# One layer of masked attention on one core: earlier order of tiles, q loads from GpSimd, later output adds, and five more tiles turned on VectorE

## The chip, the core and the metric

The kernel runs on one core of a Trainium2 chip. Its engines run side by side, each in the order of its own queue: TensorE (PE; its weight loads are PEld), VectorE (DVE), ScalarE (ACT), GpSimd (POOL) and SyncE (SP), which here only issues transfers. The metric is the device time of one execution in microseconds, as the median of several runs.

## The reference

One layer over 2708 rows of width 1024, float32. `adj` is a random 0/1 matrix with a density of 0.0014771, so that a row has four edges in the mean.

```python
h = jnp.maximum(_layernorm(x, axis=-1), 0.0)
q = h @ W_q.T + b_q
k = h @ W_k.T + b_k
v = h @ W_v.T + b_v
z = scale * (q @ k.T)
spare_z = z * adj
spare_z = jnp.where(spare_z == 0.0, -10000.0, spare_z)
attn = jax.nn.softmax(spare_z, axis=1)
out = x + jax.nn.relu(attn @ v)
```

## The kernel before

**Algebra.** W_q and W_k are multiplied into one matrix M, so that a score is (h M + b) · h', and W_v is applied after the weighted sum: a row's output is relu(u W_v + b_v) + x, where u is the weighted sum of its neighbours' h rows. Both big products (h M and u W_v) run by Strassen's scheme in Winograd's form on 512-wide halves: seven products for a pair of tiles instead of eight.

**Tiles and units.** The 2708 rows are sorted by their number of edges, within the first 1024 rows (tiles 0 to 7) and within the rest (tiles 8 to 21). A tile is 128 rows. K[t] is the number of edge slots of tile t. The hosts, tiles 0 and 8, would need 15 slots; they keep 8 (WIDE), and the slots past the 8th of their first rows make up tile 21 (SECOND), half of it for each host, with 7 slots. SECOND's sum goes through memory (`v_dram`) and is added in the host's last step.

TensorE's main loop goes over 20 units of two tiles. Units 0 to 9 are the q pairs (0,1) to (18,19). Units 10 to 19 are the output pairs, in the order in which attention finishes tiles (`order`, line 989). Tile 8 is left over (`alone`) and comes last, with four products. `multiply` (line 1044) has seven places, `after(0)` to `after(6)`, between the products of a unit; a place is written here as (unit, i). The products are s2, a12, s4, s3, then a11 and s1 of the **next** unit (`between`, `opened`), then a22. The operands s1 to s4 of the next unit are written by VectorE at (n, 2), as `put` in `blocks` (line 711).

**Turning.** A matmul needs the tile's transpose. A tile is turned in one of two ways. In the plain way TensorE does eight 128x128 transposes into PSUM (`half_turned`, line 410), and ScalarE or VectorE takes them out. A tile in `faced_tiles` goes another way: ScalarE rearranges its sum u (line 944), it is written to `u_dram`, read back in four transfers with the 32-row quarters exchanged (`by_quarters`, line 695), and VectorE transposes 32x32 blocks, a half tile in one instruction (`faces`, line 703). A tile that is not faced is either kept in SBUF (`held`) or also goes through `u_dram`. Before the change tiles 6, 5, 4, 3, 2, 0, 20, 7, 17 and 13 are faced.

**Attention.** It runs on VectorE beside the products, as a generator (`attention`, line 959) that is advanced by a planned number of microseconds, `share`, at each place (line 1277). For each slot of a tile GpSimd gathers 128 rows of h by index (line 610), VectorE multiplies with q and sums (`scores`, line 863), ScalarE takes the exponential, and VectorE adds the weighted rows into u (`sums`, line 923; ScalarE does the first slot, line 912). The gathers use 11 slots of SBUF, and two more in M from unit 10 on. A tile's q is loaded into `pq` in `fetch` (line 820): by a gather from GpSimd for tiles 0 to 7, from the SP queue for the others (line 833).

VectorE's order is written out by hand (`manual_schedule`): it is the order in which the program says things, so a planned step stands in one queue with the operands that TensorE waits for. The orders on ScalarE, GpSimd and SP are made by the framework's scheduler in the attention stage.

**W_v.** It takes the place of M when the last q products are done. Its four blocks are loaded from the SP queue (line 1259), and VectorE forms four differences of 128x2048 in T (line 1263), at places of units 9 and 10.

**Output.** `o_results` (line 1111) writes relu(u W_v + b_v) into y; GpSimd adds the x rows by an indirect transfer (`add_x`, line 1106) right after ScalarE's last write, and `send` scatters the tile to the output when the next add has been issued (line 808).

Of the kernel before, what the change touches and what calls it, by code (L numbers as in the profile page):

```python
# [18 lines left out]
P = 128  # L19
# [46 lines left out]
def tile_preln_masked_attention(  # L66
# [28 lines left out]
    HP = P // 2  # L95
    VK = K[0] - WIDE
    assert K[0] == K[EARLY] and K[SECOND] == 0 and WIDE + VK <= SLOTS
# [68 lines left out]
    mass = const.tile([P, 2], FT, name="mass")  # L166
# [17 lines left out]
    for t in HOSTS:  # L184
        nc.vector.memset(cap[:HP, t:t + 1], float(WIDE + VK))
# [448 lines left out]
    def reload(lo, hi):  # L634

        full = min(hi, FULL)
        src = tab_dram[lo >= EARLY]
        loads = [(nc.gpsimd if lo >= EARLY else nc.sync).dma_start(ptab[:, lo:full, :], src[:(full - lo) * P, :].rearrange("(t p) w -> p t w", p=P))]
        if hi > FULL:
            loads.append(nc.gpsimd.dma_start(ptab[:REST, FULL, SLOTS:], src[(FULL - lo) * P:, SLOTS:]))  # L640
        part = slice(HP, P) if lo >= EARLY else slice(0, HP)
        loads.append((nc.gpsimd if lo >= EARLY else nc.sync).dma_start(
            ptab[part, SECOND, 0:SLOTS + 1 - WIDE], src[0:HP, WIDE:SLOTS + 1]))
# [171 lines left out]
    def ask(t):  # L815

        g_of[t] = []
        wanted.extend((t, s) for s in range(K[t]))

    def fetch(t):  # L820
# [7 lines left out]
        if t == SECOND:  # L828
            assert EARLY in formed
            gather(tq[t][:HP], q_dram[:, :], t, SLOTS - WIDE, HP)  # L830
            nc.sync.dma_start(tq[t][HP:], q_late[:HP, :])
        elif t >= EARLY:
            nc.sync.dma_start(tq[t], q_late[(t - EARLY) * P:(t - EARLY + 1) * P, :])
# [5 lines left out]
    def fill():  # L839
        while wanted and free:  # L840
            t, s = wanted.pop(0)
            g = free.pop(0)
            if s == K[t]:
                half = slice(HOSTS.index(t) * HP, (HOSTS.index(t) + 1) * HP)
                nc.gpsimd.dma_start(g[:HP], v_dram[half, :])
# [29 lines left out]
    def weights(t):  # L875
# [7 lines left out]
        if t == SECOND:  # L883
# [4 lines left out]
            nc.sync.dma_start(mass[:HP, 1:2], mass[HP:, 0:1])  # L888
# [15 lines left out]
        else:  # L904
            with tc.issue_after(chain[-1].ins):
                nc.vector.scalar_tensor_tensor(w[:, :k], w[:, :k], 1.0, ok, op0=ALU.mult, op1=ALU.mult, accum_out=m[:, 1:2])
                if t in HOSTS:
                    second = HOSTS.index(t)
                    nc.vector.tensor_add(m[:HP, 1:2], m[:HP, 1:2], mass[:HP, second:second + 1])
# [4 lines left out]
            if t in HOSTS:  # L914
                assert whole_second
                wanted.insert(0, (t, k))
        us[t] = u, coef, m

    def sums(t):
        u, coef, m = us.pop(t)  # L920
        for s in range(0 if t in EMPTY else 1, K[t]):
            fill()
            chained(lambda: nc.vector.scalar_tensor_tensor(  # L923
# [4 lines left out]
        if t in HOSTS:  # L928
            chained(lambda: nc.vector.scalar_tensor_tensor(
                u[:HP], g_of[t][K[t]][:HP], m[:HP, 3:4], u[:HP], op0=ALU.mult, op1=ALU.add))  # L930
# [9 lines left out]
        if now < [unit - 2, 2] and unit <= len(q_pairs) + 4:  # L940
            faced_tiles.add(t)
        if t in faced_tiles:
# [16 lines left out]
    def attention(order):  # L959
# [11 lines left out]
        for i, t in enumerate(order):  # L971
            nxt = after[i]
            ahead = nxt is not None and K[t] + K[nxt] <= HIGH + 1
# [40 lines left out]

    def opened(n):
# [8 lines left out]
        products.append(add_block(Z, ops["s1"], T[:, 0]))  # L1024
# [19 lines left out]
    def multiply(n, results, after):  # L1044
# [7 lines left out]
        products.append(add_block(Y, ops["s2"], T[:, 1]))  # L1052
# [58 lines left out]
    def o_results(ta, tb):  # L1111
# [12 lines left out]
        def c12(Z, u2):  # L1124
# [5 lines left out]
            send(add_x(ya, ta))  # L1130
            sent.append((ya, ta))

        def c21(Y):
            nc.scalar.activation(yb[:, lo], Y, AF.Relu)  # L1134
            send(add_x(yb, tb))
            sent.append((yb, tb))
# [29 lines left out]
    sent = []  # L1166

    def send(behind):

        while sent:  # L1170
            y, t = sent.pop(0)
            with tc.issue_after(behind.ins):
                scatter(y, t, P)

    def tail(t):
        n = tiles[t][1]
        y = work.tile([P, D], FT, tag="q", name=f"y_{t}", bufs=4)
        nc.sync.dma_start(y[:n], tail_dram.to_broadcast([n, D]))
        add_x(y, t, n)
        scatter(y, t, n)  # L1180
# [9 lines left out]
    units = [("q",) + p for p in q_pairs] + [("o",) + p for p in o_pairs]  # L1190

# [19 lines left out]
    last_q = len(q_pairs) - 1  # L1211
# [13 lines left out]
    for n, unit in enumerate(units):  # L1225
# [7 lines left out]
        share = 20.9 / 7  # L1233
# [5 lines left out]
        def after(i):  # L1239
            now[1] = i  # L1240
            if (n, i) in steps_ahead:
                follow(steps_ahead[n, i])
            if (n, i) == (2, 5):
                owe(8)
                owe(9)
                rows_of[FIRST] = load_rows(units[FIRST])
# [9 lines left out]
            for at, place, src in (((-1, 0), b12, of_wv(0, 1)), ((0, 0), b11, of_wv(0, 0)), ((0, 2), T[:, 1], of_wv(1, 1)),  # L1256
# [3 lines left out]
            for at, place, a, b in (((0, 2), T[:, 0], b12, b11), ((0, 4), T[:, 1], T[:, 1], T[:, 0]),  # L1260
                                    ((1, 0), T[:, 2], b22, b12), ((1, 1), T[:, 3], b21, T[:, 1])):
# [16 lines left out]
            if nxt is not None:  # L1278
# [14 lines left out]
                if i == (2 if n in (FIRST, last_q) else 4) and n + 2 > FIRST and n + 2 < len(units) and n + 2 not in rows_of:  # L1293
# [71 lines left out]
    add_block(Z, uT[:, 0:4, :], T[:, 0])  # L1365
# [189 lines left out]
```

## Time and profile before

| | |
|---|---|
| median of 3 runs | 643.78 us (642.85, 643.78, 648.3) |
| the profiled execution, its own time | 639.94 us |
| span of its records | 638.1 us |
| mean granted TensorE clock | 0.997 |
| DMA | 176.96 MB, mean 277 GB/s |

The profile is one execution of its own, 3.84 us below the median; 1.84 us of its time lie outside the span. A row of a view names line, engine, operation and tiles; "out<-in" are the program's names with buffer numbers left out. Start times are microseconds from the span's first record. In a PE row one 128x512 float32 matmul leaves two records, so that a product of four matmuls shows as x8; a 128x128 transpose leaves one.

### The profile page before, as it was taken

What the parts mean: (1) busy time and instruction counts of PE and PEld (TensorE: products, weight loads), DVE (VectorE), ACT (ScalarE), POOL (GpSimd) and SP (SyncE); (2) the same over time, 40 slices, a digit from 0 to 9 for tenths busy, and PEclk for the clock granted to TensorE, in tenths of its full rate; (3) what the DMA queues carried; (4) which work ended last, traced back from release to release, by engine and by line L of the source; (5) the groups of instructions that cost most, each with busy time, mean ns of one, the idle gap of its engine ahead of it and who ended that gap; (6) DMA issues with size and microseconds to landing.
All of it is one profiled execution on the core that took longest, in us unless ns stands there. A gap on an engine that the chain in (4) does not pass through costs nothing.

```text
span 638.1 us, 6156 instructions
## 1 busy us (share of the span) xinstructions
PE 627.8 (98%) x1651; PEld 317.9 (50%) x1651; DVE 522.4 (82%) x1016; ACT 283.6 (44%) x423; POOL 360.2 (56%) x383
## 2 busy tenths in 40 slices
PE   9999999999999999999999999999999999999994
PEld 5777766444444444444444444444444444444441
DVE  5999888997997625999888999999999889989121
ACT  3538985849667533424342144343342432333200
POOL 2639960885768357565651663476466878633311
PEclk9999999999999999999999999999999999999998
DMA  8999997598796439996798998999999999853631
GB/s 335 407 362 321 342 351 286 200 323 330 255 379 231 171 95 317 327 323 223 233 299 289 290 414 222 295 344 311 363 382 325 325 290 291 266 145 77 187 119 50
DMA packets 60192, 176.96 MB, mean 277 GB/s; under 512 B 9799, under 2 KB 15255, under 8 KB 59512
## 3 DMA queue, kind: packets, MB, share of 16 engines
q0 software_dynamic: 25136, 78.41, 39.4%
q1 hardware_dynamic: 29514, 78.61, 35.0%
q10 hardware_dynamic: 5502, 19.48, 7.8%
q8 instruction: 15, 0.25, 0.2%
q14 instruction: 25, 0.20, 0.1%
HBM read 145.65 MB, written 40.74 MB: 292 GB/s over the span
## 4 chain that ended last, share of the span: by engine, by line
PE 90%; issue 4%; POOL 2%; DMA 2%; DVE 1%; POOLq 0%; ACT 0%; ACTq 0%; DVEq 0%
PE ps L1010 40%; PE psy L1010 29%; PE ps_y L476 6%; PE ps_x L476 4%; PE ps_z L476 4%; PE pt L415 4%; POOL g L610 2%; DMA v_dram<-u 1%; DMA M<-h_dram,tab 1%; PE ps_y L511 1%; DVE junk L863 0%; PE ps_h L1218 0%; PE ps_v L594 0%; DVE u L923 0%; DVE s L722 0%
## 5 line engine op out<-in xcount | busy, mean ns | idle before, releaser
L610 POOL DMA_INDIRECT g<-h_dram,tab x94 | 120.2, 1278 | 79.9 <-DVE u L923 30.0
L1010 PE MATMUL psy<-wlow,s 128*128 128x512 f32 x320 | 144.0, 592 | 0.0
L1010 PE MATMUL ps<-M,a 128*128 128x512 f32 x320 | 144.0, 593 | 0.0
L863 DVE SCALAR_TENSOR_TENSOR junk<-g,pq 128x1024 uint8<-128x1024 f32 x93 | 113.8, 1224 | 13.4 <-DMA g<-h_dram,tab 10.4
L1010 PEld LDWEIGHTS ps<-M,a 128*128 128x128 f32 x320 | 59.7, 190 | 70.4 <-issue 69.1
L923 DVE SCALAR_TENSOR_TENSOR u<-g,coef,u 128x1024 f32<-128x1024 f32 x69 | 88.4, 1281 | 7.0 <-ACT u L912 5.8
L1010 PEld LDWEIGHTS psy<-wlow,s 128*128 128x128 f32 x320 | 59.6, 190 | 69.2 <-issue 69.0
L389 DVE FIND_INDEX8 at<-ones,adj 128x8 uint32<-128x685 f32 (+1 forms) x88 | 74.5, 864 | 0.0
L1010 PE MATMUL ps<-wlow,s 128*128 128x512 f32 x160 | 72.0, 593 | 0.4 <-DVE s L722 0.4
L1010 PE MATMUL ps<-M,s 128*128 128x512 f32 x160 | 72.1, 592 | 0.0
L1010 PE MATMUL psy<-wlow,a 128*128 128x512 f32 x160 | 72.0, 593 | 0.0
L368 ACT ACTIVATE sized<-adj 128x2708 uint8<-128x2708 f32 (+1 forms) x22 | 54.3, 2467 | 7.4 <-DMA adj<-in_adj_dram 6.1
L298 POOL TENSOR_TENSOR hsum<-hsum,x 128x256 f32<-128x256 f32 (+1 forms) x56 | 38.6, 732 | 26.2 <-DVE wlow L444 22.5
L1109 POOL DMA_INDIRECT y<-in_x_dram,tab x19 | 34.2, 1798 | 28.9 <-ACT y L1134 12.1
L1010 PEld LDWEIGHTS ps<-wlow,s 128*128 128x128 f32 x160 | 30.3, 190 | 38.9 <-issue 38.5
L1010 PEld LDWEIGHTS psy<-wlow,a 128*128 128x128 f32 x160 | 30.3, 190 | 38.5 <-issue 37.3
L1010 PEld LDWEIGHTS ps<-M,s 128*128 128x128 f32 x160 | 30.3, 190 | 38.1 <-issue 37.4
L808 POOL DMA_INDIRECT out_dram<-y,tab x21 | 27.4, 1306 | 32.0 <-DMA y<-in_x_dram,tab 15.8
L912 ACT ACTIVATE u<-g,coef 128x1024 f32<-128x1024 f32 x18 | 20.7, 1149 | 35.8 <-DVE coef L911 35.6
L276 ACT ACTIVATE x<-x,r 128x1024 f32<-128x1024 f32 (+1 forms) x22 | 25.9, 1232 | 6.6 <-POOL r L266 6.6
L722 DVE TENSOR_TENSOR s<-a,pt 128x512 f32<-128x512 f32 x30 | 19.2, 681 | 10.9 <-ACT a L718 10.9
L476 PE MATMUL ps_y<-wlow 128*128 128x512 f32 x64 | 27.6, 592 | 0.0
(251 smaller groups left out, 843.3 us busy)
## 6 DMA issues: line engine op xcount, KB each, us to landing
adj<-in_adj_dram SPq DMA_DIRECT2D x21, 1354.0 KB, 11.5
x<-in_x_dram SPq DMA_DIRECT2D x21, 512.0 KB, 8.2
h_dram<-x ACTq DMA_DIRECT2D x21, 512.0 KB, 7.4
q_late<-q SPq DMA_DIRECT2D x12, 512.0 KB, 5.1
pq<-q_late SPq DMA_DIRECT2D x12, 512.0 KB, 6.6
u_dram<-v ACTq DMA_DIRECT2D x10, 512.0 KB, 6.4
or<-u_dram SPq DMA_DIRECT2D x40, 128.0 KB, 7.0
M<-in_wv_dram SPq DMA_DIRECT2D x4, 1024.0 KB, 8.4
```

Source lines behind the costliest of these rows:

```text
L276: nc.scalar.activation(xs[i][:n], xs[i][:n], AF.Relu, bias=r[:n, 4, i:i + 1], scale=r[:n, 3, i:i + 1])
L298: small.append(nc.gpsimd.tensor_add(hsum[:n, cols], hsum[:n, cols], xt[:n, cols]))
L368: nc.scalar.activation(sized[:n], a[:n, :, :PW], AF.Abs, accum_out=total[:n, t:t + 1])
L389: nc.vector.max_index(at[:n, k - first_k, g, :], ones[:n, 0:8], a[:n, g, :])
L415: nc.tensor.transpose(pt[:, c, :], xt[:, k * P:(k + 1) * P], ident)
L476: mm = nc.tensor.matmul(bank, a_tile(o + H * a[0], a[1], i), b(o), start=first and o == 0, stop=(o == H - 1), skip_group_check=True)
L610: return nc.gpsimd.indirect_dma_start(out=dst, out_offset=None, in_=src, in_offset=off, bounds_check=N - 1, oob_is_err=False)
L808: to = nc.gpsimd.indirect_dma_start(out=out, out_offset=bass.IndirectOffsetOnAxis(ap=ptab.bitcast(U32)[:n, t, SLOTS:SLOTS + 1], axis=0), i ...
L863: chained(lambda: nc.vector.scalar_tensor_tensor(junk, g_of[t][s], 1.0, tq[t], op0=ALU.mult, op1=ALU.mult, accum_out=zall[:, t, s:s + 1]))
L923: chained(lambda: nc.vector.scalar_tensor_tensor(u, g_of[t][s], coef[:, s:s + 1], u, op0=ALU.mult, op1=ALU.add))
L1010: mm = nc.tensor.matmul(bank, a[:, c, :], b[:, c, :], start=False, stop=(c == 3), skip_group_check=True)
L1109: return nc.gpsimd.indirect_dma_start(out=y[:n], out_offset=None, in_=x, in_offset=off, compute_op=ALU.add)
```

## The change

Seven edits are made together.

1. **Four slots.** SECOND has 4 slots instead of 7. A host's overflow is put in two parts (`OVER`): slots 8 to 11 of its first 48 or 60 rows, and slots 12 to 15 of its first 8 or 12. The second part's sum is added into the first one's by an accumulating transfer from GpSimd, issued in the host's sums; the host's `v_dram` row tile is asked for with its other slots.
2. **Order.** SECOND comes before tile 3 instead of before tile 0; the later tiles go 13, 17, 12, 18, 11, 19, 10, 15 instead of 17, 13, 18, 12, 19, 11, 15, 10.
3. **q loads.** `pq` of tiles 8 to 19 is loaded from GpSimd instead of SP.
4. **q rows.** The h rows of a q unit are gathered at (n-2, 2) instead of (n-2, 4), and the first two tiles' gathers stand ahead of two additions on GpSimd.
5. **Shares.** 22.2 us of planned steps per unit before unit 9, 17.6 in units 9 and 10, 21.2 afterwards, instead of 20.9 throughout (less 2.3 for each faced tile of the next unit, as before).
6. **Output adds.** `add_x` is issued at (n, 5) and (n+1, 1) instead of directly behind ScalarE's last write of a tile, and a tile is scattered when one more add has been issued.
7. **Turning and W_v.** Tiles 12, 18, 16, 9 and 8 are faced too, so 15 in all. Two of the four places in T are exchanged for W_v, and two of its blocks are loaded at (8, 6).

```diff
-    VK = K[0] - WIDE
+    VK = 4
+    OVER = ((48, 0), (8, 48)), ((60, 56), (12, 116))
...
         elif t >= EARLY:
-            nc.sync.dma_start(tq[t], q_late[(t - EARLY) * P:(t - EARLY + 1) * P, :])
+            nc.gpsimd.dma_start(tq[t], q_late[(t - EARLY) * P:(t - EARLY + 1) * P, :])
...
         for s in range(0 if t in EMPTY else 1, K[t]):
             fill()
+            if t in HOSTS and s == K[t] // 2 + 1:
+                rows, at = OVER[HOSTS.index(t)][1]
+                nc.gpsimd.dma_start(g_of[t][K[t]][:rows], v_dram[at:at + rows, :], accum_op=ALU.add)
...
-        if now < [unit - 2, 2] and unit <= len(q_pairs) + 4:
+        if now < [unit - 2, 2] and unit <= len(q_pairs) + 5 or unit >= len(units) - 1:
             faced_tiles.add(t)
...
-    order = [6, 5, 4, 3, 2, 0, 20, 7, 17, 13, 18, 12, 19, 11, 15, 10, 14, 1, 16, 9, 8]
+    order = [6, 5, 4, 3, 2, 0, 20, 7, 13, 17, 12, 18, 11, 19, 10, 15, 14, 1, 16, 9, 8]
-    stream = attention(order[:order.index(0)] + [SECOND] + order[order.index(0):])
+    stream = attention(order[:order.index(3)] + [SECOND] + order[order.index(3):])
...
+    def t_of(n, k):
+        return T[:, (1, 0, 2, 3)[k] if n > last_q else k]
...
-            send(add_x(ya, ta))
-            sent.append((ya, ta))
+            due.append((now[0], 5, ya, ta))
...
-            send(add_x(yb, tb))
-            sent.append((yb, tb))
+            due.append((now[0] + 1, 1, yb, tb))
...
+    def add_due():
+        while due and due[0][:2] <= tuple(now):
+            y, t = due.pop(0)[2:]
+            send(add_x(y, t), 1)
+            sent.append((y, t, P))
...
-        share = 20.9 / 7
+        share = (22.2 if n < last_q else 17.6 if n < last_q + 2 else 21.2) / 7
...
-            for at, place, src in (((-1, 0), b12, of_wv(0, 1)), ((0, 0), b11, of_wv(0, 0)), ((0, 2), T[:, 1], of_wv(1, 1)),
+            for at, place, src in (((-1, 0), b12, of_wv(0, 1)), ((-1, 6), b11, of_wv(0, 0)), ((-1, 6), T[:, 0], of_wv(1, 1)),
                                    ((0, 3), b21, of_wv(1, 0)), ((0, 4), b22, of_wv(1, 1))):
...
-            for at, place, a, b in (((0, 2), T[:, 0], b12, b11), ((0, 4), T[:, 1], T[:, 1], T[:, 0]),
-                                    ((1, 0), T[:, 2], b22, b12), ((1, 1), T[:, 3], b21, T[:, 1])):
+            for at, place, a, b in (((0, 2), T[:, 1], b12, b11), ((0, 4), T[:, 0], T[:, 0], T[:, 1]),
+                                    ((1, 1), T[:, 2], b22, b12), ((1, 2), T[:, 3], b21, T[:, 0])):
...
-                if i == (2 if n in (FIRST, last_q) else 4) and n + 2 > FIRST and n + 2 < len(units) and n + 2 not in rows_of:
+                if i == (2 if FIRST <= n < last_q - 1 or n == last_q else 4) and n + 2 > FIRST and n + 2 < len(units) and n + 2 not in rows_of:
...
             if nxt is None and i == 1:
+                uT = work.tile([P, D], FT, tag="hT", name="T_alone", bufs=2).rearrange("p (c q) -> p c q", q=P)
+                faces(uT, single["rows"], 0, DC)
+                single["turned"] = uT
+            if n == len(units) - 2 and i == 6:
                 while alone not in done:
                     advance(1.0)
-                r, = load_rows(("o", alone))
-                single["turned"] = turned(r, "alone")
+                single["rows"], = load_rows(("o", alone))
```

More of the change, by code (lines that the diff above doesn't have):

```diff
@@ L94, in tile_preln_masked_attention @@
     SECOND = NT - 1
-    HP = P // 2
-    VK = K[0] - WIDE
-    assert K[0] == K[EARLY] and K[SECOND] == 0 and WIDE + VK <= SLOTS
+    VK = 4
+    OVER = ((48, 0), (8, 48)), ((60, 56), (12, 116))
+    assert K[0] == K[EARLY] <= WIDE + 2 * VK == SLOTS and K[SECOND] == 0
+    assert sum(rows for host in OVER for rows, at in host) == P
     for t in HOSTS:
@@ L817, in ask @@
         g_of[t] = []
-        wanted.extend((t, s) for s in range(K[t]))
+        wanted.extend((t, s) for s in range(K[t] + (t in HOSTS)))
     def fetch(t):
@@ L843, in fill @@
             if s == K[t]:
-                half = slice(HOSTS.index(t) * HP, (HOSTS.index(t) + 1) * HP)
-                nc.gpsimd.dma_start(g[:HP], v_dram[half, :])
+                assert whole_second
+                rows, at = OVER[HOSTS.index(t)][0]
+                nc.gpsimd.dma_start(g[:rows], v_dram[at:at + rows, :])
             else:
@@ L972, in attention @@
             nxt = after[i]
-            ahead = nxt is not None and K[t] + K[nxt] <= HIGH + 1
+            ahead = nxt is not None and K[t] + (t in HOSTS) + K[nxt] <= HIGH + 1
             part = scores(nxt, after[i + 1]) if nxt is not None else iter(())
@@ L1240, in after @@
             now[1] = i
+            add_due()
             if (n, i) in steps_ahead:
```

63 lines of the change are left out of this document (36 added, 27 removed).

## The prediction

> **What bounds the kernel now.** I read the page first: its span, its busy times and the chain of work that ended last.
>
> ```profile
> span 638.1 us, 6156 instructions
> PE 627.8 (98%) x1651; PEld 317.9 (50%) x1651; DVE 522.4 (82%) x1016; ACT 283.6 (44%) x423; POOL 360.2 (56%) x383
> PE 90%; issue 4%; POOL 2%; DMA 2%; DVE 1%; POOLq 0%; ACT 0%; ACTq 0%; DVEq 0%
> ```
>
> TensorE is busy for 627.8 of 638.1 us and makes 90% of the chain. Busy ends are modelled for matmuls, so I asked what TensorE waited for (in total, times, longest):
>
> ```profile
> PE ps_y L511 <- POOL hsum L121: 1.2, 1, 1.2
> PE ps L1010 <- DVE s L722: 0.4, 1, 0.4
> ```
>
> That is 1.6 us in all, 1.2 of it before the first product. So nearly all of the time is TensorE's own list of work, and an edit pays only as far as it shortens that list or a wait in it. The end of the chain shows what follows the last product:
>
> ```profile
> 618.97 10.42 PE ps L1010 x24
> 629.41 0.70 DVE y_alone L1371
> 630.65 0.70 POOL out_dram L1355
> ```
>
> From 629.4 to 638.1, 8.7 us are an addition, a scatter of half a tile and its landing. The change touches none of the three. The other edits act before that, beside the products. The gain can therefore be at most the removed work on TensorE plus 0.4 us.
>
> **The turned tiles.** The timeline of TensorE in unit 17, which has two tiles turned by it:
>
> ```profile
> 545.64 1.04 PE L415 MATMUL pt<-ident,u 128*128 128x128 f32 x8
> 546.52 3.60 PE L1010 MATMUL psy<-wlow,s 128*128 128x512 f32 x8
> 549.95 1.04 PE L415 MATMUL pt<-ident,u 128*128 128x128 f32 x8
> 550.83 3.60 PE L1010 MATMUL ps<-M,a 128*128 128x512 f32 x8
> 554.26 3.60 PE L1010 MATMUL ps<-M,s 128*128 128x512 f32 x8
> ```
>
> Starts tell what the list costs, since the durations overlap: eight transposes take 546.52 - 545.64 = 0.88 us, a product 3.43. The groups of transposes in the output units, by form:
>
> ```profile
> L415 PE MATMUL pt<-ident,u 128*128 128x128 f32 x56 | 7.3, 273 | 0.0
> L415 PE MATMUL pt<-ident,or 128*128 128x128 f32 x32 | 4.2, 273 | 0.0
> ```
>
> 88 transposes are eleven tiles. The built program of the change has 40 fewer, the five tiles 12, 18, 16, 9 and 8. 5 x 0.88 = **4.4 us less on TensorE**. The mean of 273 ns holds the latency of one, not its place in the list; whoever multiplies it by 40 gets 10.9 us (a rival below). [...]
>
> **What the five tiles cost elsewhere.** A faced tile takes two block transposes on VectorE, 5 x 2 x 0.69 = 6.9 us; three slots fewer in SECOND save 3 x (1.22 + 0.08 + 1.28) = 7.7 us there, the 0.08 being the read of the sum. So VectorE's list is as long as before (the rows, with the idle time in front of a group and who ended it, behind the second bar):
>
> ```profile
> L863 DVE SCALAR_TENSOR_TENSOR junk<-g,pq 128x1024 uint8<-128x1024 f32 x93 | 113.8, 1224 | 13.4 <-DMA g<-h_dram,tab 10.4 <-DMA pq<-q_dram,tab 1.0 <-DMA pq<-q_late 0.2
> L863 DVE DVE_READ_ACCUMULATOR junk<-g,pq 128x1 f32 x93 | 7.6, 81 | 0.0
> L923 DVE SCALAR_TENSOR_TENSOR u<-g,coef,u 128x1024 f32<-128x1024 f32 x69 | 88.4, 1281 | 7.0 <-ACT u L912 5.8
> L923 DVE SCALAR_TENSOR_TENSOR u<-g,w,u 128x1024 f32<-128x1024 f32 x6 | 7.7, 1282 | 1.5 <-ACT u L889 1.4
> L705 DVE STREAM_TRANSPOSE a<-or 128x512 f32<-128x512 f32 x15 | 10.0, 694 | 1.0 <-DMA or<-u_dram 1.0
> ```
>
> Tiles 12 and 18 went through memory before; 16, 9 and 8 were kept, and now take a copy, a write and a read in quarters. The tightest is tile 8. Its last sum and the product that needs it turned:
>
> ```profile
> 586.70 1.28 DVE L929 SCALAR_TENSOR_TENSOR u<-g,m,u 64x1024 f32<-64x1024 f32 x1
> 611.82 3.60 PE L1010 MATMUL ps<-M,T_alone 128*128 128x512 f32 x8
> ```
>
> The transfers (median us to landing), and the group of the copies:
>
> ```profile
> u_dram<-v ACTq DMA_DIRECT2D x10, 512.0 KB, 6.4
> or<-u_dram SPq DMA_DIRECT2D x40, 128.0 KB, 7.0
> pq<-q_late SPq DMA_DIRECT2D x12, 512.0 KB, 6.6
> pq<-q_dram,tab POOLq DMA_INDIRECT x9, 6.9
> ```
>
> ```profile
> L944 ACT COPY v<-u 128x1024 f32<-128x1024 f32 x10 | 10.5, 1046 | 22.6 <-DVE u L923 20.7 <-DMA g<-h_dram,tab 1.8
> ```
>
> 588.0 + 1.0 + 6.4 + 7.0 + 1.4 (two faces) = 603.8, against 611.8 - 4.4 = 607.4: 3.6 us of cover, and VectorE has nothing else due in unit 19 before the first product's end. I cost it at nothing; were the cover gone, a microsecond of lateness would be one on TensorE.
>
> **VectorE's lead.** TensorE takes s1 of the next unit late in a unit; the time from VectorE's write to that product is the lead. Units 10 and 11, from the two timelines:
>
> ```profile
> 356.49 0.69 DVE L722 TENSOR_TENSOR s<-a,s 128x512 f32<-128x512 f32 x1
> 364.26 3.60 PE L1010 MATMUL ps<-wlow,s 128*128 128x512 f32 x8
> 388.19 0.69 DVE L722 TENSOR_TENSOR s<-a,s 128x512 f32<-128x512 f32 x1
> 389.03 3.67 PE L1010 MATMUL ps<-wlow,s 128*128 128x512 f32 x8 [0.36 <-DVE s L722]
> ```
>
> The lead is 364.26 - 357.18 = 7.1 us for unit 10, and 0.1 for unit 11, where the one wait is. The four W_v differences bring it down. I counted the 1024-wide attention steps that VectorE's order puts between the s1 of unit 6 and that of units 10 and 11: 59 and 71 before, 62 and 71 after. So the new shares move three steps (3 x 1.28 = 3.8 us) ahead of unit 10 and none net ahead of unit 11. SECOND's sums, no longer right behind its weights, lose the 1.4 us of idle time (ScalarE's L889 above). The leads become 7.1 - 3.8 + 1.4 = 4.7 and 0.1 + 1.4 = 1.5, before any new wait.
>
> **The W_v load is such a wait.** The SP queue's issues, the landing times of the W_v loads, and VectorE's first difference:
>
> ```profile
> 340.43 0.33 SPq L1259 DMA_DIRECT2D M<-in_wv_dram  x1
> 348.25 0.33 SPq L1084 DMA_DIRECT2D q_late<-q  x1
> 350.73 0.33 SPq L1259 DMA_DIRECT2D wlow<-in_wv_dram  x1
> ```
>
> ```profile
> DMA to landing us min/median/max: 5.2/5.4/11.6
> ```
>
> ```profile
> 351.76 2.28 DVE L1263 TENSOR_TENSOR wlow<-M 128x2048 f32<-128x2048 f32 x1
> ```
>
> Before, the block b11 went out at 340.4, ahead of a q store that waits for unit 8's last product. In the built order of the change it stands behind that store, and ScalarE's copy of tile 0's sum (1.0) stands ahead of the copy that the store waits for: an issue at 350.7 by my estimate (348.25 and a few tenths at the least). Landing takes 5.2 to 11.6, so 353.9 to 362.3, most likely 356.1. The first difference would start at 351.8 + 3.8 - 1.4 = 354.2. So VectorE waits 0 to 8.1 us, most likely 1.9; queued behind it are its own sums and the operands of units 10 and 11. Of the 1.5 us of lead at unit 11, -0.4 is left (between +1.5 and -6.6). **TensorE waits 1.0 us there in my sum** (0 to 6.6; 0.4 before), a little over the 0.4 because one landing more can be late.
>
> **q loads by GpSimd** put 14 loads into a queue that also issues the gathers. The shortest row for such an issue is 0.6 us, the nearest in kind 1.06:
>
> ```profile
> L845 POOL DMA_DIRECT2D g<-v_dram x2 | 1.2, 595 | 4.0 <-DMA v_dram<-u 4.0
> L612 POOL DMA_INDIRECT pq<-q_dram,tab x9 | 9.5, 1060 | 17.3 <-DVE junk L863 11.1 <-DMA tab<-tab_dram 4.5 <-issue 1.2
> L1109 POOL DMA_INDIRECT y<-in_x_dram,tab x19 | 34.2, 1798 | 28.9 <-ACT y L1134 12.1 <-ACT y L1126 11.4 <-issue 2.1
> ```
>
> 8 to 15 us more on an engine that is busy 56%, less three gathers. VectorE's waits for the nine q tiles that GpSimd already gathers are 1.0 us in all (the first row of L863), a ninth of a microsecond each; I take 14 x 0.11 - 0.2 = 1.3 us, spread over ten units, as hidden. [...] **The late output adds** take ScalarE's 12.1 + 11.4 us of waiting out of GpSimd's queue (L1109), ahead of gathers; a gain for VectorE's lead that I do not count. **The q rows sooner** only lengthen a lead.
>
> **Sum.** 639.94 - 4.4 + (1.0 - 0.4) = 636.1 for an execution like the profiled one. That one lies 3.84 us under the median, so I carry the difference of -3.8: 643.78 - 3.8 = **640.0 us**. "Within 1%" means 637.3 to 650.2; the three runs before alone spread by 0.8%.
>
> **Rivals.** (1) Slower than before: b11 lands late. The place is VectorE's first W_v difference in unit 9, the price 6.6 us at the 11.6 us landing: 643.78 - 4.4 - 0.4 + 6.6 = 645.6. It decides from a wait of 4.8 us on, a landing of 9.8. For: two megabytes leave together, and DMA is near full there. Against: the load alone in front took 5.4. Chance 0.13. (2) Slower by over 1%: GpSimd's q loads come late, and VectorE has no slack. In L612's row the nine q gathers stood 17.3 us behind other waits of GpSimd's queue, 1.9 each; were ten tiles' q late by that, and all of it handed on, TensorE would wait 19 us: 643.78 - 3.8 + 19 = 659.0. It makes the kernel slower from 0.4 us for each tile, by over 1% from 1.0. For: at unit 11 there is no lead to take it. Against: the 0.11 above, from the same queue. [...] Chance 0.09. (3) Faster by over 1%: a transpose costs TensorE its 273 ns, 40 x 0.273 = 10.9, so 643.78 - 10.9 + 0.6 = 633.5. Against: the 0.88 for eight. Chance 0.06. The forecast keeps 0.72.
>
> **Chances and range.** The forecast lies 2.7 us above the bound of faster, and medians of three can move by that: 0.07 of its 0.72 go there. Faster 0.06 + 0.07 = 0.13. Slower 0.09 and 0.02 of the forecast and of rival 1 together: 0.11. Same 0.76. The range runs from 637.0 (all of TensorE's waits gone, 639.0, less 2) to 647.6 (rival 1, and 2 more), the 2 being about half of what the profiled execution and the median differ by; it leaves out rivals 2 and 3.
>
> **What would show it.** Right: the plain transposes of the output units' tiles down from 88 records to 48, eight still in 0.88 us; TensorE without gaps from 1.2 to about 625; one wait of about 1 us near unit 11, ended by VectorE's s1, with idle time of VectorE before its first W_v difference, ended by that load. Wrong: TensorE waits at several units for VectorE, VectorE idle for `pq` from GpSimd (rival 2), or a wait in unit 19 for tile 8's turned rows, which would make the cover of 3.6 us too small.

## The result and the profile after

| | kernel before | changed kernel |
|---|---|---|
| median of 12 runs | 643.44 us (641.9 to 648.49) | 650.46 us (647.4 to 653.99) |
| ratio, 95% interval | | 1.0096 (1.007 to 1.0122) |
| profiled execution, its own time | 639.94 us | 651.12 us |
| TensorE's last product ends at | 629.4 us | 639.9 us |

The changed kernel is about 1% slower; the forecast was 640.0, with a range to 647.6. The page of the changed kernel, its first lines, the granted clock in 40 slices, and the chain of work that ended last by engine:

```profile
span 649.4 us, 6115 instructions
PE 629.3 (97%) x1611; PEld 316.2 (49%) x1611; DVE 526.5 (81%) x1019; ACT 285.8 (44%) x420; POOL 364.5 (56%) x397
PEclk9999999999999899999999979999999999999997
PE 40%; DVE 6%; issue 5%; DMA 2%; POOL 1%; ACT 1%; POOLq 0%; SPq 0%; DVEq 0%; ACTq 0%
```

TensorE has 40 records fewer and is still busy 1.5 us longer. Ahead of the last slice, in which the kernel ends, two slices have a digit below 9 in the clock row, the 14th and the 24th (211 to 227 and 373 to 390 us). TensorE's waits say what happens there (in total, times, longest):

```profile
PE ps_in L685 <- DVE sort L673: 3.6, 1, 3.6
PE ps L1025 <- DVE s L729: 3.0, 1, 3.0
PE pt L418 <- DMA qr<-h_dram,tab: 1.9, 1, 1.9
PE ps_y L514 <- POOL hsum L122: 1.2, 1, 1.2
PE ps L1025 <- ACT ps L767: 0.4, 1, 0.4
PE ps_x L479 <- DMA wlow<-in_wq_dram: 0.4, 1, 0.4
```

10.5 us against 1.6 before. The clock was halved twice for 6.83 us, from 222.7 and from 376.3, and TensorE was busy for 11.8 us of these; half of that, 5.9 us, is what the clock cost. The rest of its busy time is then 4.4 us shorter than before (1.5 - 5.9). Together, 8.9 us more of waits, 5.9 of half clock and 4.4 less of work are 10.4; TensorE's last product ends 10.5 us later. The removed transposes are gone as forecast (24 + 24 records for 56 + 32):

```profile
L418 PE MATMUL pt<-ident,or 128*128 128x128 f32 x24 | 3.1, 273 | 0.0
L418 PE MATMUL pt<-ident,u 128*128 128x128 f32 x24 | 3.1, 272 | 0.0
```

**The stall near 375 us.** SP's timeline, then ScalarE's, VectorE's and TensorE's:

```profile
359.44 0.34 SPq L1102 DMA_DIRECT2D q_late<-q  x1
359.87 0.45 SPq L1282 DMA_DIRECT2D M<-in_wv_dram  x1
360.42 0.45 SPq L1282 DMA_DIRECT2D wlow<-in_wv_dram  x1
360.96 14.01 SPq L707 DMA_DIRECT2D or<-u_dram  x8
375.30 0.93 SPq L1282 DMA_DIRECT2D M<-in_wv_dram  x2
```

```profile
357.88 1.04 ACT L959 COPY v<-u 128x1024 f32<-128x1024 f32 x1 [4.04 <-issue]
358.83 0.58 ACT L1117 COPY q<-psy 128x512 f32<-128x512 f32 x1
```

```profile
370.35 2.29 DVE L1286 TENSOR_TENSOR wlow<-M 128x2048 f32<-128x2048 f32 x1 [7.85 <-DMA M<-in_wv_dram]
```

```profile
377.07 6.68 PE L1025 MATMUL ps<-wlow,s 128*128 128x512 f32 x8 [3.01 <-DVE s L729]
```

It is read from the bottom: TensorE waits for s1, which stands behind the difference on VectorE, which waits 7.85 us for the W_v block b11; b11 went out right behind tile 17's q store, which waited for ScalarE's copy of q, which stood behind the copy of tile 0's sum. Then the product itself takes 6.68 us instead of 3.60. The granted clock in stretches of 3.41 us (the column behind the five engines) says why:

```profile
372.88:376.29 3.41, 1.18 (x3) 0.19 (x1) 3.38 (x6) 1.04 (x1) 1.60 (x2) 1.00 1.07 215
376.29:379.70 3.41, 2.63 (x3) 1.18 (x4) 3.34 (x5) 0.00 (x0) 0.00 (x0) 0.50 0.96 263
379.70:383.12 3.42, 3.42 (x5) 1.35 (x4) 3.42 (x5) 0.57 (x1) 0.00 (x0) 0.50 1.01 413
```

After the wait TensorE runs at half clock for a product: its records start 853 ns apart instead of 429. So the product starts 3.2 us late and the next one 6.3.

**The stall near 200 to 230 us.** GpSimd's timeline in the kernel before and in the changed one:

```profile
184.89 5.52 POOL L298 TENSOR_TENSOR hsum<-hsum,x 128x256 f32<-128x256 f32 x8
192.12 1.07 POOL L612 DMA_INDIRECT qr<-h_dram,tab  x1 [1.71 <-DMA h_dram<-x]
```

```profile
198.23 1.05 POOL L615 DMA_INDIRECT qr<-h_dram,tab  x1 [11.10 <-PE ps L1025]
199.58 0.97 POOL L615 DMA_INDIRECT qr<-h_dram,tab  x1 [0.30 <-ACT ps L767]
200.58 13.76 POOL L301 TENSOR_TENSOR hsum<-hsum,x 128x256 f32<-128x256 f32 x20
```

Before, eight small additions (tiles 8 and 9) ran while the h rows were being written, and the gathers came behind them. Now the gathers stand first, GpSimd idles 11.1 us at their head, and all twenty additions run from 200.6 to 214.3. There VectorE forms an operand from two SBUF tiles, and then TensorE wants the counts for the sort:

```profile
210.36 4.53 DVE L729 TENSOR_TENSOR s<-s,a 128x512 f32<-128x512 f32 x1
```

```profile
223.75 0.30 PE L685 MATMUL ps_in<-sort,before 128*128 128x144 bf16 x1 [3.65 <-DVE sort L673]
```

The operand takes 4.53 us instead of 0.68 and ends 0.55 us behind GpSimd's string of additions (214.89 and 214.34). The 3.85 us come back as TensorE's 3.65, and the first stretch at half clock, from 222.7, starts in that wait.

### The profile page after: what moved, and what is told of

The parts are those of the page before. It is cut to its first block, busy times and chain, and to the rows that moved or that the text cites. A ratio compares the mean times of both kernels' runs of the same rounds, so it can differ in the third digit from the quotient of the medians.

```text
span 649.4 us, 6115 instructions
## 1 busy us (share of the span) xinstructions
PE 629.3 (97%) x1611; PEld 316.2 (49%) x1611; DVE 526.5 (81%) x1019; ACT 285.8 (44%) x420; POOL 364.5 (56%) x397
## 4 chain that ended last, share of the span: by engine, by line
PE 40%; DVE 6%; issue 5%; DMA 2%; POOL 1%; ACT 1%; POOLq 0%; SPq 0%; DVEq 0%; ACTq 0%
PE ps L1025 23%; PE psy L1025 16%; DVE u L936 3%; DVE junk L873 2%; DMA M<-in_wv_dram 2%; PE pt L418 1%; DMA g<-h_dram,tab 1%; DVE s L729 1%; POOL g L613 1%; ACT u L924 0%; POOL pq L615 0%; POOL qr L615 0%; DVE q L1112 0%; DVE y_alone L1397 0%; POOL out_dram L1381 0%
## 5 line engine op out<-in xcount | busy, mean ns | idle before, releaser
L1025 PE MATMUL psy<-wlow,s 128*128 128x512 f32 x320 | 146.1, 599 | 0.0
L613 POOL DMA_INDIRECT g<-h_dram,tab x91 | 115.5, 1269 | 52.9 <-issue 18.6
L873 DVE SCALAR_TENSOR_TENSOR junk<-g,pq 128x1024 uint8<-128x1024 f32 x90 | 110.0, 1223 | 9.1 <-DMA g<-h_dram,tab 7.6
L936 DVE SCALAR_TENSOR_TENSOR u<-g,coef,u 128x1024 f32<-128x1024 f32 x70 | 89.7, 1282 | 7.5 <-ACT u L924 6.2
L1025 PE MATMUL ps<-wlow,s 128*128 128x512 f32 x160 | 75.0, 613 | 3.0 <-DVE s L729 3.0
L1127 POOL DMA_INDIRECT y<-in_x_dram,tab x19 | 31.2, 1644 | 29.9 <-ACT y L1144 20.8
L815 POOL DMA_INDIRECT out_dram<-y,tab x21 | 25.4, 1211 | 15.6 <-DMA y<-in_x_dram,tab 5.6
L959 ACT COPY v<-u 128x1024 f32<-128x1024 f32 x15 | 15.7, 1046 | 40.6 <-DVE u L936 30.4
L729 DVE TENSOR_TENSOR s<-a,pt 128x512 f32<-128x512 f32 x26 | 16.7, 682 | 15.9 <-remote 7.7
```

Source lines behind the costliest of these rows:

```text
L613: return nc.gpsimd.indirect_dma_start(out=dst, out_offset=None, in_=src, in_offset=off, bounds_check=N - 1, oob_is_err=False)
L729: step = (eng or nc.vector).tensor_tensor(ops[name], a, b, op=op)
L815: to = nc.gpsimd.indirect_dma_start(out=out, out_offset=bass.IndirectOffsetOnAxis(ap=ptab.bitcast(U32)[:n, t, SLOTS:SLOTS + 1], axis=0), i ...
L873: chained(lambda: nc.vector.scalar_tensor_tensor(junk, g_of[t][s], 1.0, tq[t], op0=ALU.mult, op1=ALU.mult, accum_out=zall[:, t, s:s + 1]))
L936: chained(lambda: nc.vector.scalar_tensor_tensor(u, g_of[t][s], coef[:, s:s + 1], u, op0=ALU.mult, op1=ALU.add))
L1025: mm = nc.tensor.matmul(bank, a[:, c, :], b[:, c, :], start=False, stop=(c == 3), skip_group_check=True)
```

## The experiments

The experiments ran on four chips (1 to 4, 5 to 8, 9 to 12 and 13 to 16), and the kernel before was measured on each: 643.35, 644.95, 640.34 and 640.78 us. So kernels are compared on one chip, and over chips only by their ratio to it.

**1 to 4: the two stalls, one by one.** In 1 the gathers go back behind the additions:

```diff
-                rows_of[FIRST] = load_rows(units[FIRST])
                 owe(8)
                 owe(9)
+                rows_of[FIRST] = load_rows(units[FIRST])
```

> The changed kernel with one thing undone: at (2,5) the gathers of the first q unit's rows stand behind GpSimd's additions of tiles 8 and 9 again. Theory A (two stalls, each with its own place: GpSimd's additions pushed into VectorE's operands near 210 us, and the W_v block b11 late near 370 us; both longer by a stretch at half clock): the stall near 200 to 230 us goes, 2.1 + 3.8 + 1.9 = 7.8 us, so about 650.5 - 7.8 = 642.7; the wait near 370 us stays with its half clock, about 7. Rival B (the adj and h writes landed late in that one execution, the order is innocent): no change, about 650. Rival C (q loads by GpSimd are what costs): no change, about 650.

In 2 the first two W_v loads are issued where unit 8's last result is stored, ahead of tile 17's store (in place of the two entries at (8, 6)):

```diff
             nc.scalar.copy(qb[:, lo], Y)
+            if (ta, tb) == q_pairs[-2]:
+                nc.sync.dma_start(M[:, 0, 0], of_wv(0, 0))
+                w_load = nc.sync.dma_start(T[:, 0], of_wv(1, 1))
...
-            store(qb, tb)
+            with tc.issue_after(w_load.ins) if (ta, tb) == q_pairs[-2] else nullcontext():
+                store(qb, tb)
```

> The changed kernel with one thing moved: the loads of b11 and of the W_v block in T stand ahead of the store of tile 17's q on the SP queue. Theory A: the load goes out when TensorE has read M's first block, some 9 us sooner, VectorE's wait of 7.85 us before its first W_v difference goes, and with it TensorE's wait of 3.2 and the half-clock stretch of 3.4 to 3.8: about 650.5 - 7.0 = 643.5. Rival D (the load lands late wherever it is issued, DMA being full there, or the new shares leave VectorE no lead at unit 10 anyway): the wait stays, 648 to 651.

3 has both edits; 4 is the kernel before with the opposite of edit 1.

> Both of the other two edits together on the changed kernel. Theory A: both stalls go and what is left is the sum of the forecast, TensorE's list less the five turned tiles: 650.5 - 7.8 - 7.0 = 635.7, between 634 and 639, faster than before by 0.7 to 1.4%; TensorE's gaps below 3 us in all. Rival C (q loads, order and shares cost besides): 641 or more, with other waits of TensorE.

> The kernel before with one line moved: the gathers of the first q unit's rows stand ahead of GpSimd's additions of tiles 8 and 9, as in the change. Theory A: slower, by 4 to 8 us (647 to 651), with a VectorE operand of some 4.5 us near 210 us while GpSimd adds, and a wait of TensorE for the sort's operand. Rival B (only late landings of that execution): no change, 643.

| | median us | ratio to before, 95% |
|---|---|---|
| 1 gathers behind additions | 646.62 | 1.0047 (1.0014 to 1.0079) |
| 2 two W_v blocks ahead | 649.45 | 1.0076 (1.0045 to 1.0106) |
| 3 both | 642.51 | 0.998 (0.9951 to 1.0008) |
| 4 before, additions behind gathers | 647.82 | 1.0085 (1.0051 to 1.0119) |

The additions are a cause: 4 alone makes the kernel before 0.85% slower, as expected, and TensorE waits 3.2 us for the sort. In 1 the wait for the sort is gone, but TensorE still waits for the first gathered rows (2.2 us), and the mean granted clock of its profile is 0.987, against 0.984 in the changed kernel; by the ratios it wins 0.5%, some 3.2 us, where 7.8 were expected. Experiment 2 missed: the wait for s1 went, and two others came. TensorE's waits of experiment 2:

```profile
PE ps_in L685 <- DVE sort L673: 3.4, 2, 2.8
PE pt L418 <- DMA qr<-h_dram,tab: 2.5, 1, 2.5
PE ps L1024 <- DMA M<-in_wv_dram: 2.4, 1, 2.4
PE psy L1024 <- DVE q L1108: 2.4, 1, 2.4
```

The second pair of W_v blocks was next in line. It stands on SP behind the reads of unit 11's rows (14.01 us in SP's timeline above), which wait for tile 3. Tile 3 comes later in the new order. And 3 stays 7 us above the 635.7 that was expected; TensorE's waits of it still hold 1.8 us for a W_v block and 2.3 for the first gathered rows; the rest was not traced.

**5 to 8: what a usual execution is, the turned tiles alone, the rest of W_v.** 5 is the kernel before, unchanged. 6 is the kernel before with the larger faced set and tile 8's early read, and nothing else of the change. 7 is 3 with

```diff
-                if i == (2 if FIRST <= n < last_q - 1 or n == last_q else 4) and n + 2 > FIRST and n + 2 < len(units) and n + 2 not in rows_of:
+                if i == (2 if FIRST <= n < last_q - 1 else 4) and n + 2 > FIRST and n + 2 < len(units) and n + 2 not in rows_of:
```

so that all four blocks stand ahead of those reads. 8 is 3 with the faced set of before.

> The kernel before, unchanged, profiled a second time. The first profile had TensorE without a gap, 639.94 us, while the median of its timed runs is 643.4. Theory E (a typical execution of the kernel before has waits too, of late adj and h transfers near 200 us, and the first profile was a lucky one): TensorE waits of 1 to 4 us in all beside the 1.6 of the first, time 641 to 645. Rival (the waits at the first rows of the q units come from the change alone): no such wait, 640.

> The kernel before with the five more tiles faced and nothing else of the change (tile 8 with its early read and late faces as there). Theory A (the turned tiles are worth what the list says, the rest of the change costs): 643.4 - 4.4 = 639.0, between 637.5 and 640.5; 40 transposes fewer, no new wait of TensorE over 1 us. Rival F (VectorE, with 6.9 us of block transposes more and none of its other work removed, or the round trip of tiles 9 and 8, hands the gain back): 642 to 646, with TensorE waiting for VectorE's s1 in units 11 to 15 or for the faces in unit 19.

> The third experiment's kernel with one more place moved: the reads of unit 11's rows are asked for at (9,4) instead of (9,2), so that the last two W_v blocks stand ahead of them on the SP queue (the reads wait for tile 3, which the new order finishes later). Theory A2 (what was left of the stall is the same kind: loads queued behind a step that waits): TensorE's waits near 377 us (1.95) and VectorE's of 4.4 before its third difference go; 642.5 - 2 = 640.5, between 639 and 641.5. Rival D (DMA is full there, the loads land late anyway): 642 to 643.

> The third experiment's kernel with the five tiles turned by TensorE again (the faced set of the kernel before). It prices that edit alone at this place: by the list 5 x 0.88 = 4.4 us more, so 642.5 + 4.4 = 646.9. Rival G (a transpose costs its recorded 273 ns): 642.5 + 10.9 = 653.4. Rival F (the faces hand the gain back on VectorE): 642 to 644.

| | median us | ratio to before, 95% |
|---|---|---|
| 5 kernel before, one execution | 643.85 | |
| 6 before, five tiles faced | 650.96 | 1.008 (1.0054 to 1.0105) |
| 7 both, all W_v blocks ahead | 642.37 | 0.9959 (0.9933 to 0.9984) |
| 8 both, tiles not faced | 648.02 | 1.0055 (1.0025 to 1.0084) |

TensorE's waits in 5, the kernel before on another chip:

```profile
PE psy L1010 <- DVE q L1091: 2.8, 1, 2.8
PE pt L415 <- DMA qr<-h_dram,tab: 1.4, 1, 1.4
PE ps_y L511 <- POOL hsum L121: 1.2, 1, 1.2
PE ps L1010 <- DVE s L722: 0.4, 1, 0.4
```

The first profile of the kernel before had none of these waits in the middle: it was a good execution, or one of the kind in which the h writes go out early (at 180.2 us; 183.9 in 5; last section). Experiment 6 missed both its expectations: the five tiles alone cost more than they save. VectorE has 6.9 us more to do and nothing less, which is the likely reason and no tested one. Its only profile is of an execution 8 us above its median, so it tells which places are short, not what each costs; one of them is tile 8, whose faces come late, with another stretch at half clock (the product takes 5.95 us, not 3.60, and the slice from 624 to 641 us has a 7 in the clock row):

```profile
628.05 5.95 PE L1010 MATMUL ps<-M,T_alone 128*128 128x512 f32 x8 [4.95 <-DVE T_alone L705]
```

Experiment 7 came out at 642.37, above the 639 to 641.5 that were expected; by the ratios it gains 0.2% on 3, within the noise, and its profile has no wait for a W_v block left. 8 is 5.6 us slower than 7. Less the step from 3 to 7, which 8 lacks too (some 1.3 us by the ratios), about 4.3 are left for the five tiles inside the change, against 4.4 by the list.

**9 to 12.** 9 is the changed kernel with both W_v moves and its additions left where the change has them. 10, 11 and 12 are 7 with one line changed each:

```diff
-            nc.gpsimd.dma_start(tq[t], q_late[(t - EARLY) * P:(t - EARLY + 1) * P, :])
+            nc.sync.dma_start(tq[t], q_late[(t - EARLY) * P:(t - EARLY + 1) * P, :])
...
-        share = (22.2 if n < last_q else 17.6 if n < last_q + 2 else 21.2) / 7
+        share = 20.9 / 7
...
-                (2, 2): "p16", (2, 3): "p17 a8 k8 z",
+                (2, 2): "p16", (2, 3): "a8 k8 p17 z",
```

> The changed kernel with both moves of the seventh experiment (all four W_v blocks ahead of the steps that wait on the SP queue) and GpSimd's additions left behind the gathers as in the change. The second experiment moved only the first two blocks and won 1 us where 7 were expected; its trace shows two new waits of 2.5 us, for VectorE and for a W_v block. Theory A2 (the four blocks are one queue, and the last two were next in line): the waits near 377 and 387 us go too, 649.5 - 4.5 = 645. Rival D (DMA full there): 648 to 650.

> The seventh experiment's kernel with the q loads of tiles 8 to 19 on the SP queue again (SECOND's stay on GpSimd). Rival C (q loads by GpSimd cost VectorE 0.4 to 1.9 us for each tile, as the prediction's second rival): faster, 636 to 640. Theory H (they cost nothing from GpSimd, and on SP, where they wait for a free buffer, they hold up the stores, reads and W_v blocks behind them): 643 to 650, with TensorE waits near units 9 and 10.

> The seventh experiment's kernel with 20.9 us of planned steps per unit throughout, as before the change. In the sixth experiment the five faced tiles alone, without the new shares, made VectorE finish tile 8 so late that TensorE waited 5.1 us for its faces and ran 3 us at half clock. Theory I (the shares pay for the faced tiles): tile 8 finishes some 5 to 10 us later, its faces make TensorE wait in unit 19, 642.4 + 2 to 8 = 644 to 650. Rival J (the four slots alone make up for the faces): no wait there, 641 to 643.

> The seventh experiment's kernel with ScalarE's last three h tiles ahead of a count of adj (2.5 us) in its queue, so that the last h rows are written sooner. Every profile but the first of the kernel before has TensorE waiting 1.6 to 2.7 us near 201 us for the first gathered rows. Theory K (that wait hangs on ScalarE's queue, where the count waits for an adj tile): the wait goes, 642.4 - 1.8 = 640.6. Rival L (it hangs on the landing of the write and the gather; or the count, now later, holds up adj tiles and the sort): 642 to 645.

| | median us | ratio to before, 95% |
|---|---|---|
| 9 W_v blocks ahead only | 637.92 | 0.9957 (0.9942 to 0.9972) |
| 10 q loads on SP | 635.95 | 0.9923 (0.991 to 0.9937) |
| 11 shares of before | 637.80 | 0.9973 (0.9951 to 0.9995) |
| 12 h rows ahead of a count | 639.97 | 0.9995 (0.9984 to 1.0007) |

On this chip the kernel before takes 640.3, so the expected times, made on the chips before, can't be held against these, and 7 was not run on it. 11 against 10 (which should run like 7, see 16) puts the new shares at some 2 us, at the low end of what was expected, but without the wait for tile 8's faces that was to cost them. In 12 TensorE waits 2.0 us for the sort, as its rival had it, and the mean granted clock of its profile is 0.992, against 0.995 in 11; that the moved count holds up adj tiles is argued only, and the wait that 12 was to remove shows in none of these four profiles. Whether 10's lead came from the q loads needed one chip for all.

**13 to 16: one chip, four kernels.**

> The changed kernel, unchanged, on the same chip as the three kernels sent with it. The chips differ: in the last call the kernel before took 640.3 us, where it had taken 643.4 and 645.0 in the calls before, and a kernel with GpSimd's additions behind the gathers was faster than before there. Theory M (the change's two stalls are waits for transfers, so they shrink where transfers land sooner): on a chip where the kernel before takes 640, the ratio is between 1.000 and 1.007; where it takes 644, 1.007 to 1.012. Rival (the stalls hang on the order of the queues alone): 1.007 to 1.012 on any chip.

> The seventh experiment's kernel again (GpSimd's additions ahead of the gathers, all four W_v blocks ahead on the SP queue), beside the changed kernel on the same chip. Theory A: ratio to before 0.993 to 0.997; below the changed kernel by 0.7% or more on any chip, since both stalls are orders of queues.

> The ninth experiment's kernel again (only the W_v blocks moved), on the same chip. It splits the difference between the changed kernel and the one before in this list: theory A puts 7 us on W_v and 4 to 8 on the additions where transfers are late, and 1 to 4 on the additions where they are early (the trace of the ninth showed 2.5 and 1.7 us at the sort).

> The tenth experiment's kernel again (the second one of this list, with the q loads of tiles 8 to 19 on the SP queue). Rival C (q loads by GpSimd cost time): faster than the second of this list by 1 us or more on the same chip. Theory H (they cost nothing): within 0.2% of it, and what the tenth gained over the others of its call was those others' own losses.

| | median us | ratio to before, 95% |
|---|---|---|
| kernel before | 640.78 | |
| 13 changed kernel | 642.57 | 1.0029 (1.0016 to 1.0041) |
| 15 W_v blocks ahead | 636.37 | 0.993 (0.9917 to 0.9943) |
| 14 and additions ahead of the gathers | 635.73 | 0.992 (0.9906 to 0.9934) |
| 16 and q loads on SP | 635.50 | 0.9936 (0.9914 to 0.9958) |

This splits the change: the order of the W_v loads (all four blocks moved together) 6.2 us, the additions 0.6 on this chip, which is hardly clear of the noise and less than the 1 to 4 that were expected, the q loads nothing that the medians show (0.2 us, the ratios' intervals overlap). Two of TensorE's waits in 13, then the changed kernel's VectorE and SP here, and the same of 14:

```profile
PE ps L1024 <- DVE s L729: 3.0, 1, 3.0
PE psy L1024 <- DVE wlow L1285: 0.9, 1, 0.9
```

```profile
361.60 2.29 DVE L1285 TENSOR_TENSOR wlow<-M 128x2048 f32<-128x2048 f32 x1 [7.64 <-DMA M<-in_wv_dram]
```

```profile
351.33 0.45 SPq L1281 DMA_DIRECT2D M<-in_wv_dram  x1
```

```profile
353.61 2.28 DVE L1289 TENSOR_TENSOR wlow<-M 128x2048 f32<-128x2048 f32 x1
```

```profile
342.39 0.35 SPq L1118 DMA_DIRECT2D M<-in_wv_dram  x1
354.12 3.76 SPq L1285 DMA_DIRECT2D M<-in_wv_dram  x2
```

Issued 8.9 us sooner, the block is there when VectorE comes to it at 353.6. Its landing took 11.2 us there at most; whether it was any shorter than in 13 is not on record, and need not have been. All waits of TensorE in 14 of 0.2 us and more:

```profile
PE ps_y L514 <- POOL hsum L122: 1.2, 1, 1.2
PE psy L1024 <- DVE q L1108: 0.2, 1, 0.2
```

The operand beside GpSimd's additions is shorter on this chip, too: in the changed kernel's order it ends 0.55 us behind them, and they begin at 194.9 us in 13 and at 195.3 in 15, against 200.6 in the changed kernel's first profile. In 13, 15 and 14 it reads:

```profile
207.84 1.38 DVE L729 TENSOR_TENSOR s<-s,a 128x512 f32<-128x512 f32 x1
```

```profile
207.59 2.02 DVE L729 TENSOR_TENSOR s<-s,a 128x512 f32<-128x512 f32 x1
```

```profile
207.60 0.68 DVE L729 TENSOR_TENSOR s<-s,a 128x512 f32<-128x512 f32 x1
```

14 beats both kernels, by 0.8% and 1.1% on this chip; the same kernel as 7 was 0.4% faster than before on another.

## Why the prediction was wrong

Two steps failed, and both are waits of TensorE that the sum had at 1.0 us and at nothing: the landing of the W_v load, and the gathers moved ahead of GpSimd's additions. Behind each of them stood a stretch at half clock (6.83 us), which the sum did not have either. The removed work was as forecast.

**What bounds the kernel**: right, but the clock is a third term. TensorE's last product ends where its list, its waits and its time at half clock put it: without the latter two it would end at 627.8 us in the kernel before and at 623.4 in the changed one. That the profiled execution had almost no waits was read as the kernel's habit; experiment 5 shows 4.2 us of waits in the middle in another execution. The 3.8 us between profile and median were carried along without asking what they were made of.

**The turned tiles**: right. The list loses 4.4 us by these two figures, and with the waits taken out kernel 14 runs 640.78 - 635.73 = 5.05 us under the kernel before, against 4.4 + 0.4 in the sum's bound "all of TensorE's waits gone". The rival of 273 ns for each transpose, 10.9 us, is out.

**What they cost elsewhere**: right for this change (in the changed kernel tile 8's faces ended at 614.6, its product started at 622.3). It rests on the other edits: in the one profile of experiment 6, which has the five tiles alone, TensorE waits 4.95 us for these faces. Experiment 11 shows that it isn't the new shares that keep the cover; which edit does was not tried.

**VectorE's lead**: the size was right. 4.7 us of lead were worked out for unit 10, less a wait of 7.64 gives -2.9; TensorE waited 3.0 us there in run 13. That the wait would show at unit 11 was wrong: it showed at unit 10, and 0.9 us more in front of the second difference.

**The W_v load: the first step that failed.** The mechanism, the store ahead of b11, was right, and so was the place: an issue at 350.7 was worked out and 351.33 measured in run 13, and VectorE's arrival 354.2 against 353.96. The landing was mis-sized: 5.4 us, the median, was taken as most likely, out of a row that went to 11.6. It took 361.60 - 351.33 = 10.3. The row holds three landings only; two of the five W_v loads before have none on record, b11's own among them. Its 11.6 us are those of a block with a second one 1.4 us behind it, and in the change b11 has one 0.5 us behind it; its 5.4 are those of a block alone. Besides, nine gathers of half a megabyte leave just ahead of b11 in the changed kernel, from 338.6 to 352.5 in run 13. That the second block or the gathers make the landing long is argued; no run took them away. And TensorE's wait was priced at 1 us for 1 us, which leaves out the half clock behind it. The W_v loads cost 6.2 us (15 against 13) instead of the 1.0 in the sum; of these the profile of 13 shows 3.0 + 0.9 us of waits and 1.5 of half clock (the product behind the first wait takes 5.06 us instead of 3.60). This is the prediction's first rival, which had 0.13. Its 645.6 less the 3.0 between the two medians of the kernel before (643.78 and 640.78) is 642.6 for that chip, where 642.57 was measured, but that is luck: its 6.6 us were one wait, and what was measured is that wait at 3.0 and the half clock, the second wait and the sort's 0.6 beside it.

**"The q rows sooner only lengthen a lead": the second step that failed.** The sum had nothing for it. The gathers were moved past two steps of GpSimd's own queue, and what waits at the head of that queue holds what follows (GpSimd idles 11.1 us there in the changed kernel, with all twenty additions behind it). Two rows of the kernel before show how little was needed; VectorE's last step for the sort's operand, and TensorE's product that reads it:

```profile
216.81 0.31 DVE L666 TENSOR_TENSOR sort<-deg,down 128x144 bf16<-128x144 f32 x1
```

```profile
217.18 0.24 PE L678 MATMUL ps_in<-sort,before 128*128 128x144 bf16 x1
```

Done at 217.12, used at 217.18: no lead at all, in a stage that the prediction did not look at since no wait stood there. In the first profile of the changed kernel it costs 3.65 us of waiting and 2.9 of half clock; by medians 0.6 us on one chip (14 against 15), and 0.5% (1 against the changed kernel, by their ratios) and 0.85% (experiment 4) on the first chip. The 1.9 us that TensorE waits for the gathered rows themselves are not this edit's alone: the kernel before has 1.4 of them in experiment 5.

**q loads by GpSimd**: nearly right to cost them at nothing (16 against 14). But there is a price in **the tail**, which was costed as untouched. From TensorE's end to the span's end it is 9.5 to 9.9 us in every profile with the q loads on GpSimd, the changed kernel's among them, and 8.7 in 10 and 16, which have them on SP, as in the kernel before (9.05 in 6). So some 0.9 us of the end go with this edit, though the medians of 14 and 16 differ by 0.2 only. The prediction read these 8.7 us as an addition, a scatter and its landing; the scatter has landed at 633.1 in the kernel before, and most of the rest is a closing step of GpSimd's queue that takes 6.37 us there and 6.87 in the changed kernel. Why it takes longer was not tried. **The late output adds, the order of the tiles and the four slots** were not tried by themselves.

## What to carry to other kernels

A load is worth looking at with its whole queue: who stands in front of it, what that one waits for, and how long transfers take just there, not in the median. A lead of zero is a wait that has not shown yet, and one profile without waits does not tell how often it does; the places to list are those where an operand is ready just as it is used. An edit that removes work from the bounding engine pays only with the edits that keep its suppliers on time, so such parts are measured together and one by one.

## What the runs showed of the hardware

**Two waits of TensorE cost twice in the changed kernel, and two in experiment 2 only once.** Behind the wait at 374 us in the changed kernel seven records in a row started about 853 ns apart (the first 986) instead of 429, 3.1 us more in all. In its trace the granted clock changes at 222.69, 229.52, 376.29, 383.12 and 642.53 us, whole multiples of 3.413 us from one another (2, 43, 2 and 76), so that both stretches at half clock ahead of the last product are two such steps long. With the time up to the last product cut into these steps, TensorE was idle for 2.59 us in the step ahead of the first of the two (219.28 to 222.69), for 2.23 in the one ahead of the second (372.88 to 376.29), and for 1.35 us at most in every other step at full clock. Two waits of 2.4 us in experiment 2 fell into steps with 1.85 us of idle time, and with 1.26 and 1.11, and cost nothing more: the clock is 1.00 there, the product behind the first of them takes 3.70 us, and the clock row of that run has a 9 in each slice from 211 to 633 us (TensorE's busy time stands behind the comma, the clock third from the end):

```profile
378.58:381.99 3.41, 1.56 (x4) 0.85 (x5) 2.81 (x13) 0.86 (x3) 0.00 (x0) 1.00 1.05 358
385.41:388.82 3.41, 2.15 (x6) 0.60 (x4) 2.78 (x5) 0.80 (x2) 1.59 (x2) 1.00 0.98 355
388.82:392.23 3.41, 2.30 (x6) 1.10 (x7) 0.00 (x0) 0.00 (x0) 0.00 (x0) 1.00 1.00 413
```

That the cutting into steps decides, and where between 1.85 and 2.23 us the limit would lie, is read from these few steps and was not tried.

**VectorE's operand from two SBUF tiles took longer while GpSimd added.** 4.53, 2.02 and 1.38 us (the changed kernel, 15 and 13) instead of 0.68, each ending 0.55 us behind GpSimd's string of additions, while two operands with one source in PSUM took their usual time beside the same additions (the pair just ahead of it in the changed kernel):

```profile
209.16 1.28 DVE L729 TENSOR_TENSOR s<-a,pt 128x512 f32<-128x512 f32 x2 [0.36 <-ACT a L725]
```

The 4.53 us span six of GpSimd's additions, of 0.7 us each. What holds the operand is not shown.

**The groups of runs differ in when the last h writes go out.** The first of the last three was issued at 184.9 us in the changed kernel, 185.0 in experiment 2, 184.7 in 3, 183.9 in 5 and 185.4 in 6; in 13 and 15 all three had gone out by 183. The kernel before took 643 to 645 us on the chips of the former and 640.8 on that of the latter. The changed kernel lost 1.0% where the kernel before takes 643.4, and 0.3% where it takes 640.8. By this sign (180.2 us) the first profile of the kernel before, on which the prediction rests, is of the second kind, while the median of its timed runs, 643.4, is like the first. That it is the chip, and not some other difference between the groups of runs, is not shown.
